# A two-layer graph network on one Trainium2 core: the second half of the first edge pass gathers float32 rows

## The chip, the core and the metric

The kernel runs on one core of one Trainium2 chip. A core has five engines that run side by side, each through its own instructions in order: PE (TensorE, matrix products), DVE (VectorE), ACT (ScalarE), POOL (GpSimd, which here issues the gathers) and SP (SyncE, which here issues the other DMAs). They wait for each other by semaphores. The metric is the device time of one execution in microseconds (us); lower is better.

## The reference: what is computed

The graph has 6250 nodes of 256 float32 features and 100,000 edges, sorted by destination. The edges crowd at low destinations, since `dst` is the square of a uniform number. Cut to what matters:

```python
def layer0(x, src, dst, weight, bias):                       # mean over the neighbours, then a linear layer
    agg = segment_sum(x[src], dst, n) / maximum(deg, 1)
    out = concatenate([x, agg], -1) @ weight
    return out / norm(out) + bias

x = layernorm(x + layer0(x, src, dst, ...))
x = layernorm(x + layer1(x, src, dst, ...))                  # the same edge sums again, then a mixture of 64 experts
```

The change touches only `segment_sum(x[src], dst)` of the first layer, the *first edge pass*.

## The kernel before, in words

**Two ways to sum edges.** The edges are cut into 782 chunks of 128. The first 288 chunks (dense destinations) become a matrix of edge counts, `adj_a` and `adj_b`, which later is multiplied by the node rows (`dense_product`, L420 to L444, product at L432). The other 494 chunks are *gathered*: an indirect DMA on POOL (`gather_rows`, L394 to L396) fetches the 128 source rows of a chunk, and PE multiplies them by a one-hot matrix that says which destination of a window each edge has. A group of 4 to 16 chunks shares one window and one accumulator `po`.

**Rows in three parts.** PE multiplies bfloat16 in one pass and float32 in several. So `three` splits every node row into three bfloat16 parts that add up to the float32 value, and writes them to `x3_rows` (1536 bytes a row instead of 1024). The first 64 steps (up to `xch`) can't wait for that table: they gather float32 rows from `x` with a float32 one-hot (`edge_rows`, L600 to L608) and one product (L667). From then on a chunk is gathered from `x3_rows` and takes three bfloat16 products with one bfloat16 one-hot (L685). Those one-hots are made four at a time by one DVE instruction (`near4`, L414 to L418). In both forms they are made `ahead = 4` steps early. There are eight row buffers, so POOL can be eight chunks ahead of PE.

**The order of the work.** The pass is one loop over the 494 steps (one gathered chunk each) inside a region in which the order of PE, DVE, ACT and SP is what the program wrote; POOL has little but gathers there. Side work is put between the steps by hand: `Track` spreads a list of work over a range of steps, `Steps` runs things some steps later. The side work by step, in `work`:

- up to step 318: the counts of the dense part and the degrees;
- 240 to 374: the dense product over `adj_a`; 322 to 374 also `by_destination` (L819, 392 very small products);
- 377 to 470: the dense product over `adj_b`; its node tiles `x3d` (192 KB) are loaded on SP (L896) into three buffers;
- from 321 on: the first layer itself (`layer1`, L504 to L570), one tile of 128 nodes every 3.5 steps (`B_GAP`), as soon as its edge sums are complete. It loads `xw` and `xb`, multiplies (L521), normalizes (ACT L535, L536, L546, L551; DVE L527 to L549), stores `x1_rows` (L552), splits the result in three parts (ACT L557, L564; DVE L561, L566) and stores them to `h3_rows` (L569; two buffers, so L557 of one tile waits for the store of the tile two before). ACT also clears the finished sums (L868).

At the end of a group, `group_end` copies `po` (ACT, `sums`, L632), PE transposes it three steps later (L402), DVE adds it to `acc` (L409). The last 8 groups (from group 46, step 457 on) do this with no lag. The second edge pass gathers `h3_rows`, so it begins when the last tile of the first layer has been stored.

Per step PE is given, in this order: the products of the step's chunk, then what `work` adds. ACT and DVE get the one-hot of the chunk four steps ahead first, then the rest.

Of the kernel before, what the change touches and what calls it, by code (L numbers as in the profile page):

```python
# [9 lines left out]
F32 = mybir.dt.float32  # L10
F16 = mybir.dt.float16
BF16 = mybir.dt.bfloat16
I32 = mybir.dt.int32
AF = mybir.ActivationFunctionType
OP = mybir.AluOpType
# [4 lines left out]
P = 128  # L20
N = 6250
D = 256
# [11 lines left out]
ACH, DCH = 216, 288  # L34
# [12 lines left out]
OHB = 4  # L47
# [13 lines left out]
def edge_groups(c0, c1, width, most):  # L61


    groups = []
    while c0 < c1:
        g = 1
        while g < min(most, c1 - c0):
            e0, e1 = c0 * P, (c0 + g + 1) * P
            per = E * E / (2.0 * N * e1)
            if N * (e1 / E) ** 2 - N * (e0 / E) ** 2 + 1 + 5 * (e1 - e0) ** 0.5 / per > width:  # L70
                break
            g += 1
        groups.append((c0, g))
        c0 += g
    return groups
# [4 lines left out]

FINE = 24
GGRP = edge_groups(DCH, NCH - FINE, P, 16) + edge_groups(NCH - FINE, NCH, P, 4)

AT_ONCE = max(i for i, (_, g) in enumerate(GGRP) if g >= 7)

# [60 lines left out]
def gnn_moe_kernel(  # L146
# [22 lines left out]
    nc = tc.nc  # L169
# [38 lines left out]
    ones = const.tile([P, P], F32, name="ones")  # L208
# [16 lines left out]
    with ExitStack() as gctx:  # L225
# [168 lines left out]
        def gather_rows(r, table, index):  # L394
            nc.gpsimd.indirect_dma_start(out=r, out_offset=None, in_=table,  # L395
                                         in_offset=bass.IndirectOffsetOnAxis(ap=index, axis=0))  # L396
# [186 lines left out]
        with ExitStack() as c:  # L583
# [4 lines left out]
            while GGRP[xgrp][0] - DCH < FIRST:  # L588
                xgrp += 1
            xch = GGRP[xgrp][0]  # L590
            assert xch <= DCH + FIRST + 16
            bufs = []
            rsq_out = wk.tile([P, NT], F32, name="rsq_out", bufs=1)
# [2 lines left out]
            steps = Steps()  # L596
            complete = [-1]
            free = dict(LAYER)

            def edge_rows(pool, ch, dt):  # L600
                oh = pool.tile([P, P], dt, name="oh")
# [35 lines left out]
            def gathered():  # L637
                ahead = 4
                ready = []

                def more_rows(ch):
                    if ch >= NCH:
                        return
                    i = ch - DCH
                    if ch < xch:
                        ready.append(edge_rows(ohf, ch, F32))
                    else:
                        if i % OHB == 0 or near_now[0] is None:
                            near_now[0] = near4(ohp, i - i % OHB)
                        ready.append(near_now[0][:, :, i % OHB])  # L650

                near_now = [None]
                with tc.tile_pool(name="stf", bufs=1, side="right") as stf, \
                        tc.tile_pool(name="ohf", bufs=6, side="right") as ohf:
                    bufs_f = [stf.tile([P, D + 1], F32, name=f"rows{i}") for i in range(7)]
                    for b in bufs_f:
                        nc.vector.memset(b[:, D:], 1.0)
                    for i in range(ahead):
                        more_rows(DCH + i)
                    for g_, (c0, g) in enumerate(GGRP[:xgrp]):  # L660
                        po = ps2.tile([P, D + 1], F32, name="po")
                        for ch in range(c0, c0 + g):
                            r = bufs_f[ch % 7]
                            gather_rows(r[:, :D], x, src_i[:, ch : ch + 1])
                            if ch + ahead < xch:
                                more_rows(ch + ahead)
                            nc.tensor.matmul(po, ready.pop(0), r, start=(ch == c0), stop=(ch == c0 + g - 1))  # L667
                            if ch == c0 + g - 1:
                                group_end(g_, po)
                            yield ch - DCH  # L670
                for i in range(ahead):
                    more_rows(xch + i)
                for g_, (c0, g) in enumerate(GGRP):
                    if g_ < xgrp:
                        continue
                    po = ps2.tile([P, D + 1], F32, name="po")
                    for ch in range(c0, c0 + g):
                        r = bufs[ch % nbuf]
                        gather_rows(r[:, : 3 * D], x3v, src_i[:, ch : ch + 1])
                        more_rows(ch + ahead)  # L680
                        oh = ready.pop(0)

                        for s in (2, 0, 1) if ch == c0 else (0, 1, 2):
                            w = D + (s == 2)
                            nc.tensor.matmul(po[:, :w], oh, r[:, s * D : s * D + w], start=(ch == c0 and s == 2),  # L685
                                             stop=(ch == c0 + g - 1 and s == 2))
                        if ch == c0 + g - 1:
                            group_end(g_, po)
                        yield ch - DCH
# [187 lines left out]
            with tc.manual_schedule(engines=ordered), ExitStack() as c1:  # L877
# [24 lines left out]
                def work(i):  # L902
                    nonlocal due, wl, psl, ohp, dense_done
                    if i == X_END + 9:
                        cx.close()
                        st = c1.enter_context(tc.tile_pool(name="st", bufs=1))
                        for k in range(nbuf):
                            bufs.append(st.tile([P, 3 * D + 1], BF16, name=f"rows3{k}"))
                            nc.vector.memset(bufs[k][:, 3 * D :], 1.0)
                        ohp = c1.enter_context(tc.tile_pool(name="ohp", bufs=3))  # L910
                        psh = hold.enter_context(tc.tile_pool(name="psh", bufs=1, space=PSUM))
                        ph[0] = psh.tile([P, NT], F32, name="ph")
                        ohc = hold.enter_context(tc.tile_pool(name="ohc", bufs=3))
                        psx = ca.enter_context(tc.tile_pool(name="psx1", bufs=1, space=PSUM))
                        psa[0] = ca.enter_context(tc.tile_pool(name="psa", bufs=3, space=PSUM))
                        wx = ca.enter_context(tc.tile_pool(name="wx", bufs=2))
                        every = counts(ohc, psa)
                        tracks.append(Track(every[:ACH], i, A_END - 4))
                        tracks.append(Track(every[ACH:], A_END + 1, END - 4))
                        tracks.append(Track([lambda t=t: staged(steps, own(wx, psx, t)) for t in range(NT)],  # L920
                                            i + 4, A_END - 12))
                        tracks.append(Track(sources(ohc), i + 8, END - 4))
                    if i == A_END:
                        ca.close()
                        psa[0] = cb.enter_context(tc.tile_pool(name="psb", bufs=2, space=PSUM))
                        tracks.append(dense(DA_END, adj_a, DENSE, 0))
                    if i == END:
                        cb.close()
                        with tc.tile_pool(name="psf", bufs=1, space=PSUM) as psf:
                            out_degrees(ph[0], psf)  # L930
                        hold.close()
                        wl = c1.enter_context(tc.tile_pool(name="wl", bufs=2))
                        psl = c1.enter_context(tc.tile_pool(name="psl", bufs=1, space=PSUM))
                        psg = cg.enter_context(tc.tile_pool(name="psg", bufs=1, space=PSUM))
                        tracks.append(Track(by_destination(psg), END + 4, DA_END))
                    for v in tracks:
                        v.at(i)
                    if i == DA_END + 3:
                        dense_done = EDGE // P
                        cd.close()  # L940
                        cg.close()
                        tracks.append(dense(DB_END, adj_b, MORE, EDGE))
                    if i == DB_END + 3:
                        dense_done = ND
                        cd.close()
                    if i > END + 2 and i >= due:
                        for t in todo:
                            if TLAST[t] <= complete[0] + 1 and (t >= ND or t < dense_done):
                                first_layer(t, wl, psl)
                                todo.remove(t)  # L950
                                due = max(due, i - 2) + (B_GAP if i < NG - 8 else 1)
                                break
                    steps.advance()
# [774 lines left out]
```

## Time and profile before

| What | Value |
|---|---|
| median of 4 runs | 2203.29 us (2199.85 to 2208.48) |
| the profiled execution | 2196.67 us |
| its span, first to last instruction | 2194.9 us |
| mean granted TensorE clock | 0.904 of full speed |
| PE busy | 1709.4 us (78%) |
| DVE / ACT / POOL busy | 1076.3 (49%) / 607.9 (28%) / 1208.1 us (55%) |
| first gather of the first edge pass | at 7.7 us |
| gather of step 332 / of the last step, 493 | at 520.42 / at 780.14 us |
| last store to `h3_rows` | at 817.3 us |

How to read it: busy times are sums over the whole span, and say little of a stage. The views used below are cut by time instead: busy time and clock of each engine in a stretch, who waited for whom in it (total us, times, longest), the DMA queues in it, and the instructions in order of time. An engine's "idle before" is put down to what ended it, its *releaser*.

### The profile page before, as it was taken

The page shows a single profiled execution, that of the slowest core. Times are in us where ns is not written, and L with a number is a line of the kernel's source. Part 1 is how long each engine was busy: PE and PEld are TensorE (multiplying, and loading weights), DVE is VectorE, ACT ScalarE, POOL GpSimd, SP SyncE. Part 2 cuts the span into 40 slices and gives each one's busy share as a digit, 9 for nine tenths or more (in the row PEclk, how much of TensorE's full clock was granted, in tenths as well). Part 3 has the DMA queues.
Part 4 walks back from the last instruction along what each step waited for, and adds up shares of the span by engine and source line. Part 5 has one row for each costly group of instructions (what it writes and reads, how often), then busy time and mean ns, then how long its engine had stood idle before and what let it go on. Part 6 is the DMA issues. An engine that isn't in the chain of part 4 may idle for free. (4 is left out here: it accounts for less than half of the span.)

```text
span 2194.9 us, 33723 instructions
## 1 busy us (share of the span) xinstructions
PE 1709.4 (78%) x9269; PEld 1207.1 (55%) x9341; DVE 1076.3 (49%) x4063; ACT 607.9 (28%) x1617; POOL 1208.1 (55%) x1391
## 2 busy tenths in 40 slices
PE   4688877788888738788667767766669998999797
PEld 2366555556655425454445444444347876787573
DVE  7666677675677661000245554535532233222398
ACT  8511235333444340000022222212212221222125
POOL 7766666666566516566666666666235554554100
PEclk8598899999999969999888899988869999999899
DMA  6766665567899836666666655555268887877353
GB/s 219 269 173 180 176 176 173 168 174 217 261 289 304 255 124 211 197 190 187 192 194 190 191 159 164 162 153 151 84 208 303 300 302 262 269 247 251 109 162 118
DMA packets 242215, 445.32 MB, mean 203 GB/s; under 512 B 35695, under 2 KB 165480, under 8 KB 242015
## 3 DMA queue, kind: packets, MB, share of 16 engines
q0 software_dynamic: 71808, 211.15, 32.9%
q1 hardware_dynamic: 167886, 230.37, 31.9%
q10 hardware_dynamic: 2320, 1.51, 0.2%
q8 instruction: 79, 1.29, 0.2%
q14 instruction: 122, 0.99, 0.2%
HBM read 377.20 MB, written 70.89 MB: 204 GB/s over the span
## 5 line engine op out<-in xcount | busy, mean ns | idle before, releaser
L395 POOL DMA_INDIRECT rows<-h_rows,src_i x494 | 477.7, 967 | 264.4 <-issue 101.3
L395 POOL DMA_INDIRECT rows<-x_rows,src_i x430 | 429.4, 999 | 246.0 <-issue 85.1
L1220 PE MATMUL both_po<-rows,oh 128*128 128x256 bf16 x1482 | 233.2, 290 | 124.8 <-ACT sums L1225 55.7
L1220 PEld LDWEIGHTS <-oh 128*128 128x128 bf16 x1482 | 166.3, 117 | 180.3 <-issue 143.4
L417 DVE TENSOR_TENSOR oh<-iota_lo,near 128x512 bf16<-128x512 bf16 x232 | 99.3, 430 | 306.7 <-PE both_po L1220 167.6
L685 PE MATMUL po<-rows,oh 128*128 128x256 bf16 (+1 forms) x1290 | 224.5, 287 | 3.5 <-issue 2.5
L1491 POOL DMA_INDIRECT core<-ob,ix x100 | 101.5, 1015 | 200.7 <-DVE ob L1490 184.9
L1489 PE MATMUL po<-w2t,h 128*128 128x256 f32 x800 | 190.7, 388 | 1.0 <-ACT h L1482 0.5
L1482 ACT ACTIVATE h<-ph,b1c 128x128 f32<-128x128 f32 (+1 forms) x288 | 94.4, 410 | 335.8 <-PE ph L1480 160.5
L779 PE MATMUL pa<-oha,ohl 128*128 128x490 bf16 x288 | 111.7, 394 | 77.8 <-issue 28.6
L1489 PEld LDWEIGHTS po<-w2t,h 128*128 128x128 f32 x800 | 150.3, 192 | 38.9 <-ACT h L1482 16.2
L685 PEld LDWEIGHTS <-oh 128*128 128x128 bf16 x1290 | 138.2, 119 | 49.1 <-issue 10.5
L1490 DVE TENSOR_TENSOR ob<-po,b2b 128x256 f32<-128x256 f32 x100 | 42.4, 424 | 227.2 <-PE po L1489 208.8
L758 DVE TENSOR_SCALAR oha<-iota_h,rel 128x490 bf16<-128x490 f16 x288 | 103.1, 366 | 96.7 <-PE po L685 38.1
L409 DVE TENSOR_TENSOR acc<-acc,pt 128x256 f32 x108 | 45.3, 420 | 151.2 <-PE both_po L1220 35.7
L1468 PE MATMUL ph<-xt,w1t 128*128 128x256 f32 x448 | 118.8, 406 | 0.0
L1225 ACT COPY sums<-both_po 128x256 f32<-128x256 f32 x54 | 20.1, 371 | 355.4 <-remote 209.1
L1468 PEld LDWEIGHTS ph<-xt,w1t 128*128 128x128 f32 x448 | 110.6, 326 | 5.6 <-issue 2.6
L1448 POOL DMA_INDIRECT xb<-xx_tok,ix x100 | 98.9, 989 | 25.0 <-issue 23.3
L432 PE MATMUL pd<-adj_b,x 128*128 128x448 bf16 x294 | 109.3, 372 | 1.7 <-issue 0.8
L432 PE MATMUL pd<-adj_a,x 128*128 128x512 bf16 x274 | 109.9, 401 | 0.7 <-issue 0.7
L1473 PE MATMUL ph<-w1t,xt 128*128 128x512 f32 x176 | 88.6, 604 | 0.5 <-DVE xt L1461 0.5
(343 smaller groups left out, 3363.4 us busy)
## 6 DMA issues: line engine op xcount, KB each, us to landing
w1t<-in_L_gnn_w_dram SPq DMA_DIRECT2D x72, 512.0 KB
w2t<-in_L_gnn_w_dram SPq DMA_DIRECT2D x72, 512.0 KB
x3d<-x_rows SPq DMA_DIRECT2D x98, 192.0 KB
core<-zero SPq DMA_DIRECT2D x7, 1792.0 KB
ys<-core SPq DMA_DIRECT2D x48, 256.0 KB
h_rows<-h SPq DMA_DIRECT2D x49, 192.0 KB
x<-h_rows SPq DMA_DIRECT2D x49, 192.0 KB
x_rows<-x SPq DMA_DIRECT2D x24, 384.0 KB
```

What stands on the lines that cost most here:

```text
L395: nc.gpsimd.indirect_dma_start(out=r, out_offset=None, in_=table, in_offset=bass.IndirectOffsetOnAxis(ap=index, axis=0))
L417: nc.vector.tensor_tensor(oh, iota_lo, near[:, None, c0 : c0 + OHB].to_broadcast([P, P, OHB]), op=OP.is_equal)
L432: nc.tensor.matmul(pd[h, w], side(x3, s, h), adj[:, t, a:b], start=(t == 0 and s == 0), stop=(t == NT - 1 and s == 2))
L685: nc.tensor.matmul(po[:, :w], oh, r[:, s * D : s * D + w], start=(ch == c0 and s == 2), stop=(ch == c0 + g - 1 and s == 2))
L758: nc.vector.tensor_scalar(oha, iota_h, rel[:, ch : ch + 1], None, op0=OP.is_equal)
L779: nc.tensor.matmul(pa[0].rearrange("p t w -> p (t w)"), low, places.pop(ch), start=first, stop=last)
L1220: nc.tensor.matmul(po, oh, r[:, :, s, :], start=(ch == c0 and s == 0), stop=(ch == c0 + g - 1 and s == 2))
L1448: nc.gpsimd.indirect_dma_start(out=xb[:, h, :], out_offset=None, in_=xx_tok, in_offset=bass.IndirectOffsetOnAxis(ap=ix[:, 0, h : h + 1], a ...
L1468: nc.tensor.matmul(ph[:, hc], w1m[:, c, hc, :], xt[:, c], start=(c == 0), stop=(c == 1))
L1482: nc.scalar.activation(h1[:, hc].rearrange("p h m -> p (h m)"), pre[hc].rearrange("p h m -> p (h m)") if k == 0 else pre[hc], AF.Gelu, bia ...
L1489: nc.tensor.matmul(po, h1[:, hc, h, :], w2t[:, hc * D : (hc + 1) * D], start=(hc == 0), stop=(hc == 3))
L1491: i = nc.gpsimd.indirect_dma_start(out=core, out_offset=bass.IndirectOffsetOnAxis(ap=ix[:, 1, h : h + 1], axis=0), in_=ob[:, h, :], in_off ...
```

## The change

From the first group that begins at step 326 or later, which is step 332 (`tgrp`, `tch`), to the end of the pass at step 493, a chunk is gathered as the 128 float32 rows of `x` (1024 bytes each) and takes one float32 product 257 columns wide, whose last column, set to one, counts the edges. That is 162 chunks. Their one-hots are float32 too, so a buffer that held four bfloat16 one-hots now holds two: `plain_rows` makes two at a time, the first on ACT by two activations (Abs, Relu), the second on DVE by one comparison, after a DVE copy of the two columns of places. The row buffers are seen as float32; their column of ones is set by DVE at each buffer's first use (8 times). The dense products and the second edge pass still use the three-part tables.

```diff
+PLAIN = 326
...
+            tgrp = next(g_ for g_, (c0, _) in enumerate(GGRP) if c0 - DCH >= PLAIN)
+            tch = GGRP[tgrp][0]
...
+            def plain_rows(c0):
+                v = ohp.tile([P, P, OHB], BF16, name="oh4").rearrange("p a b -> p (a b)").bitcast(F32)
+                place = ohp.tile([P, 2], F32, name="place2")
+                i = c0 - DCH
+                nc.vector.tensor_copy(place, near[:, i : i + 2])
+                two = [v[:, k * P : (k + 1) * P] for k in range(2)]
+                nc.scalar.activation(two[0], iota_row, AF.Abs, bias=place[:, 0:1], scale=-1.0)
+                nc.scalar.activation(two[0], two[0], AF.Relu, bias=ones[:, 0:1], scale=-1.0)
+                nc.vector.tensor_scalar(two[1], iota_row, place[:, 1:2], None, op0=OP.is_equal)
+                return two
...
-                    if ch < xch:
+                    if ch >= tch:
+                        if (ch - tch) % 2 == 0:
+                            ready.extend(plain_rows(ch))
+                    elif ch < xch:
...
+                        if g_ >= tgrp:
+                            r = r[:, : 2 * (D + 1)].bitcast(F32)
+                            if ch < tch + nbuf:
+                                nc.vector.memset(r[:, D:], 1.0)
+                            gather_rows(r[:, :D], x, src_i[:, ch : ch + 1])
+                            more_rows(ch + ahead)
+                            nc.tensor.matmul(po, ready.pop(0), r, start=(ch == c0), stop=(ch == c0 + g - 1))
+                            if ch == c0 + g - 1:
+                                group_end(g_, po)
+                            yield ch - DCH
+                            continue
...
-                            bufs.append(st.tile([P, 3 * D + 1], BF16, name=f"rows3{k}"))
+                            bufs.append(st.tile([P, 3 * D + 2], BF16, name=f"rows3{k}"))
```

## The prediction

> **What bounds the kernel now.** I read the times by stage first, since the page's shares are means over the whole span. Columns: stretch, length, then busy time of PE, PEld, DVE, ACT and POOL, the granted clock, the DMA engines' share, GB/s.
>
> ```profile
> 520.00:590.00 70.00, 63.41 (x613) 46.19 (x625) 44.71 (x169) 30.73 (x96) 42.19 (x44) 0.93 0.84 253
> 590.00:745.00 155.00, 128.09 (x793) 88.67 (x793) 110.49 (x418) 72.74 (x232) 96.37 (x99) 0.98 0.91 291
> 745.00:800.00 55.00, 32.15 (x151) 21.82 (x149) 36.71 (x138) 25.09 (x79) 20.04 (x21) 0.81 0.55 170
> ```
>
> The changed steps lie here. Step 332 is gathered at 520.4 us, and the three stretches are stage A (dense product over `adj_a`, 42 changed steps), B (over `adj_b`, 99 gathers in it) and C (no dense product, the remaining 21). In A, PE is busy 63.4 of 70 us at a clock of 0.93: PE is the bound. In B nothing is full: PE is idle 27 us of 155, the DMA engines are at 0.91. In C every engine is half idle, so a chain of waits sets the time. The second pass starts after the last store to `h_rows` at 817 us, so what these stages lose or gain is passed on whole.
>
> Next, who waits in B: PE's waits, then those of ACT, then of POOL.
>
> ```profile
> PE pd L432 <- DMA x3d<-x_rows: 13.9, 14, 2.1
> PE pg L830 <- DVE mv L544: 4.2, 1, 4.2
> PE pt L402 <- issue: 3.5, 4, 1.1
> PE pd L432 <- issue: 3.4, 6, 1.0
> ```
>
> ```profile
> ACT h L557 <- DMA h_rows<-h: 21.1, 10, 4.7
> ACT h L557 <- issue: 20.7, 13, 3.7
> ```
>
> ```profile
> POOL rows L395 <- PE po L685: 26.2, 25, 3.0
> ```
>
> PE waits 17.3 us in front of L432, nearly all for node tiles of the dense product, and never for gathered rows: POOL is the one that waits for PE to free a row buffer. ACT stands 42 us in front of L557, until an old store of `h` has landed. So traffic costs something in B, but not through the gathers' own arrival.
>
> **The change, part by part.**
>
> *Products.* The trace has both kinds, in the same stretch (start, length, engine, line):
>
> ```profile
> 661.47 0.73 PE L432 MATMUL pd<-adj_b,x3d 128*128 128x448 bf16 x3
> 662.04 1.03 PE L521 MATMUL po<-w,acc 128*128 128x256 f32 x4
> 662.90 0.49 PE L685 MATMUL po<-rows,oh 128*128 128x256 bf16 x3
> 663.23 0.73 PE L432 MATMUL pd<-adj_b,x3d 128*128 128x448 bf16 x3
> ```
>
> From start to start, three bfloat16 products of 256 columns take 663.23 - 662.90 = 0.33 us. Two float32 products of 256 columns (four records) take 662.90 - 662.04 = 0.86, so one takes 0.43. "One in place of three" is therefore 0.10 us longer, not shorter. Divided by the clock: A 42 x 0.10/0.93 = 4.5 us, B 99 x 0.10/0.98 = 10.1, C 21 x 0.10/0.81 = 2.6, together **+17 us** of PE. All of it is on the path in A. In B it can be paid for by PE's idle time only if the waits that make that idle time get shorter.
>
> A float32 weight load is longer too (row L521, mean 205 ns, against 118 ns in row L685), but L521's 0.86 us already holds its loads, so they are hidden behind products. The Trainium skill, page "TensorE: Matmul & The Clock Gate", section "Weight-path perf modes", says that the fast weight load is off for FP32 inputs. That speaks against the change; if nothing hid the loads, two of 0.2 us a chunk would add 65 us to the sum. The pair of L521 shows that they are hidden.
>
> *Traffic.* The queue of the gathers, in B and in the opening stretch from 45 to 97 us, where rows are float32:
>
> ```profile
> q0 software_dynamic: 6311, 19.38, 40.7%
> ```
>
> ```profile
> q0 software_dynamic: 1734, 4.75, 28.7%
> ```
>
> A three-part gather costs 0.407 x 16 x 155 / 99 = 10.2 engine-us, a float32 one 0.287 x 16 x 52 / 37 = 6.5. B saves 99 x 3.7/16 = 23 us of DMA time, and its share falls from 0.91 to (141 - 23)/155 = 0.76. What that buys is the 17.3 us at L432, between 0 (if SP, where each `x3d` load stands behind stores that wait for ACT, is what makes them late) and 17.3. The nearest row is stage A: at a share of 0.84 PE waits 0.2 us there for the same loads, though it uses them a third more slowly. I take **-12 us**. POOL's cost per gather stays, 0.95 us and 0.3 between two; that floor of 1.25 a step lies under today's 155/99 = 1.57.
>
> *One-hots.* Before, DVE makes four in 0.42 us (L417) with room for twelve. Now each pair takes two ACT instructions, one DVE copy and one DVE comparison, with room for six. The opening stage shows the prices:
>
> ```profile
> L607 ACT ACTIVATE oh<-oh,ones 128x128 f32<-128x128 f32 x36 | 14.5, 402 | 2.5 <-ACT oh L606 1.4
> L606 ACT ACTIVATE oh<-iota_row,rel 128x128 f32<-128x128 f32 x36 | 14.3, 396 | 5.5 <-PE po L667 3.9 <-issue 1.7
> L604 DVE TENSOR_SCALAR oh<-iota_row,rel 128x128 f32<-128x128 f32 x24 | 6.5, 270 | 2.6 <-PE po L667 2.2 <-issue 0.4
> ```
>
> Two activations take 0.73 us from one pair's start to the next one's (19.03 to 19.76 us). So ACT gets 81 x 0.73 = 59 us of work, 36 of it in B: from 72.7 to 109 of 155 (0.70). DVE loses 25 x 0.42 = 10 us in B and gets 50 x (0.27 + 0.15 for the copy, as in rows of that size) = 21: from 110 to 121 (0.78). Both have the time on average. But these engines go through their lists in order, and the one-hots now stand behind L557's waits for a store of up to 4.7 us, while PE is only four steps (some 6 us) away. What is late then is the product itself and, behind it on PE, the dense products. The nearest row is the opening stage (8 to 98 us), where the same one-hots are made with ACT 64.3/90 = 0.71 and DVE 70.2/90 = 0.78 busy, just the shares worked out above. There PE waited 5.6 us for `oh` and 5.7 for another ACT result in front of the product, 11.3 us in 61 chunks. All of that on 162 chunks is 30 us; the lower end is 0, since ACT's 42 us at L557 can take in the 36. The longest of those waits fell in the first loads, so I take less than half: **+12 us**.
>
> The skill has a rule against this, page "ScalarE: Activation LUTs", section "Rules for kernel authors": take VectorE, not ScalarE, for relu and its like. The rows agree in direction (0.73 us against 0.27). By that rule the pair would cost DVE 22 us more and ACT nothing; the sum here goes by what was written.
>
> *The rest.* Eight settings of the column of ones stand on DVE in the step that uses them, not four ahead; DVE is idle 25 of 70 us in A, so 0 to 3 us. In C, `sums` (L632) stands behind a pair of activations at the end of 6 groups, and PE waits for `sums` there already; but ACT makes the pair while PE does the group's last product, so 0 to 6 x 0.73 = 4 us. I take **+1** for both together. ACT's function tables don't change: the built order of the changed kernel has five table loads, as before has. SP's and POOL's orders are the same.
>
> *Sum:* 17 - 12 + 12 + 1 = **+18 us**. The profiled execution took 2196.67 us (span 2194.9), so it would be 2214.7. It lies 6.6 us under the median of the runs, 2203.29; added to that, the forecast is **2221 us**.
>
> **The rivals.**
>
> *Faster: traffic is the real bound of B.* The waits at L557 and L432 are both waits for transfers and hold up ACT, SP and PE alike. If they go, and the one-hots fit into the freed time of ACT, all 27 us of PE's idle time in B can go: -27 + 17 = -10 us, with a few us more if the modelled ends of the products hide idle time, 2190 us. For it: 0.91 in B. Against it: in A, PE pays with nothing to gain, and each x3d load also waits on SP. It decides if PE's wait at L432 disappears and none for `oh` takes its place.
>
> *No change.* The price of the products (17) is just met by the wait at L432 (17.3), and ACT's idle time takes in the one-hots: 2203.
>
> *Slower by far: ACT becomes the bound.* If the wait at L557 doesn't shrink by what ACT now does in between, ACT adds its work to the path: 36 us in B and up to 15 in A and 8 in C, 59 in all; with the 17 of the products partly beside it, some 45 us, 2248. It decides from the point at which ACT's new 0.37 us a step no longer fits into its idle time, 82 of 155 us in B, of which 42 are at L557.
>
> *That it doesn't do what it says* is ruled out: the built order has 162 float32 products and 162 gathers from `x` in place of 486 and 162.
>
> **How the numbers follow.** Forecast (+8 to +35) 0.48, faster 0.20, no change 0.20, ACT-bound 0.12. About 0.3% (6.6 us) is what a measurement of this kernel can tell from no change. So faster 0.20, same 0.20, slower 0.60. The range goes from inside the faster case, 2192, to the ACT-bound price, 2248, and leaves out about half of each of these two.
>
> **What would show it.** In the profile after: a product of `oh4` 0.43 us from start to start, not 0.33; gathers of 6.5 engine-us; a DMA share near 0.76 in the stage of `adj_b`; PE's wait for `x3d` down to about 5 us; a new wait of PE for `oh` on ACT or DVE of 10 to 15 us; ACT at 0.7. The forecast is wrong if PE doesn't wait for one-hots (then it is the no-change case, or faster), or if ACT hardly has idle time left (then the slow one).

## The result, and the profile after

The changed kernel takes 2213.92 us (median of 40 runs, 2201.56 to 2224.34), the kernel before 2206.26 us beside it (66 runs). The ratio is 1.0035 [1.0024, 1.0045]: slower by 7.7 us, where +18 was forecast. The profiled execution took 2213.0 us (span 2211.3, clock 0.907).

Lines have moved: in the changed kernel the dense product is L434, the plain product L704, the copy of places L609, Abs and Relu L611 and L612, the comparison L613, the `h` activations of the first layer L559 and L566, `sums` L648, the transpose L404. Step 332 is gathered at 525.6 us, so the stages lie at 525 to 597 (A), 597 to 755 (B) and 755 to 812 (C). Busy times by stage (stretch, length, PE, PEld, DVE, ACT, POOL, clock, DMA share, GB/s):

```profile
525.00:597.00 72.00, 65.15 (x571) 45.68 (x582) 48.63 (x207) 44.69 (x136) 41.27 (x43) 0.98 0.69 206
597.00:755.00 158.00, 137.46 (x691) 92.91 (x693) 121.20 (x492) 105.35 (x329) 94.55 (x99) 0.97 0.81 246
755.00:812.00 57.00, 36.38 (x135) 25.45 (x132) 40.48 (x158) 33.78 (x105) 20.05 (x21) 0.83 0.45 138
```

PE has 9 us more work in B, ACT 33 more, DVE 11 more, and the DMA engines 0.10 less: all of it near what was worked out (ACT 105.35/158 = 0.67, DVE 0.77). Yet every stretch is longer by only 2 or 3 us, 7 in all. PE's waits in B:

```profile
PE pg L860 <- DVE col L859: 4.4, 1, 4.4
PE pd L434 <- DMA x3d<-x_rows: 3.8, 5, 1.8
PE pt L404 <- ACT sm L548: 3.1, 2, 1.9
PE pt L404 <- issue: 2.3, 2, 1.5
PE pd L434 <- issue: 2.0, 2, 1.6
```

The wait for node tiles fell from 17.3 to 5.8 us, as forecast. A wait of the product L704 for a one-hot, which was forecast with 10 to 15 us, isn't there in B. In A there is one, of 1.7 us, and one for which the profile shows no releaser (the same view for 525 to 597 us):

```profile
PE po L704 <- issue: 2.7, 1, 2.7
PE po L704 <- DVE place L609: 1.7, 1, 1.7
```

ACT's waits in B, and then from C to the start of the second pass:

```profile
ACT h L559 <- DMA h_rows<-h: 13.6, 8, 3.8
ACT h L559 <- issue: 5.9, 7, 3.2
ACT oh L611 <- issue: 5.8, 5, 2.0
ACT oh L611 <- PE pd L434: 4.3, 2, 2.2
ACT oh L611 <- DVE place L609: 4.0, 3, 2.4
ACT oh L611 <- DVE sm L550: 3.6, 3, 2.0
```

```profile
ACT h L559 <- DMA h_rows<-h: 9.8, 5, 2.6
ACT oh L611 <- DVE place L609: 7.7, 4, 3.0
```

Here is the new thing. ACT's 42 us in front of the first `h` activation shrank to 19.5, and in part of their place ACT stands in front of its own Abs, 17.7 us in the four rows above. Of these, 7.6 are put to DVE (the copy of the places, or what DVE does ahead of it), 4.3 to PE, and 5.8 to nothing that the profile shows. The prices of the parts, from the order of PE's instructions in B and from the gathers' queue in the same stretch:

```profile
641.37 0.73 PE L434 MATMUL pd<-adj_b,x3d 128*128 128x448 bf16 x3
641.93 0.60 PE L704 MATMUL po<-rows,oh 128*128 128x257 f32 x2
642.37 0.73 PE L434 MATMUL pd<-adj_b,x3d 128*128 128x448 bf16 x3
```

```profile
q0 software_dynamic: 4743, 12.97, 30.3%
```

A float32 product takes 642.37 - 641.93 = 0.44 us from start to start (forecast 0.43). A gather takes 0.303 x 16 x 158/99 = 7.7 engine-us (forecast 6.5, before 10.2).

### The profile page after: what moved, and what is told of

Its sections match the earlier page's. It is cut to its first block, busy times and chain, and to the rows that moved or that the text cites. A ratio compares the mean times of both kernels' runs of the same rounds, so it can differ in the third digit from the quotient of the medians.

```text
span 2211.3 us, 33835 instructions
## 1 busy us (share of the span) xinstructions
PE 1723.0 (78%) x9108; PEld 1212.0 (55%) x9179; DVE 1094.4 (49%) x4192; ACT 663.2 (30%) x1779; POOL 1198.8 (54%) x1391
## 5 line engine op out<-in xcount | busy, mean ns | idle before, releaser
L397 POOL DMA_INDIRECT rows<-x_rows,src_i x268 | 267.6, 998 | 152.1 <-issue 51.1
L397 POOL DMA_INDIRECT rows<-in_x_dram,src_i x226 | 226.6, 1003 | 136.6 <-PE po L704 53.7
L1250 PEld LDWEIGHTS <-oh 128*128 128x128 bf16 x1482 | 167.4, 118 | 190.0 <-issue 154.0
L419 DVE TENSOR_TENSOR oh<-iota_lo,near 128x512 bf16<-128x512 bf16 x191 | 82.5, 434 | 307.4 <-PE both_po L1250 166.9
L809 PE MATMUL pa<-oha,ohl 128*128 128x490 bf16 x288 | 110.5, 388 | 86.6 <-issue 40.3
L715 PE MATMUL po<-rows,oh 128*128 128x256 bf16 (+1 forms) x804 | 140.0, 285 | 2.3 <-issue 1.9
L411 DVE TENSOR_TENSOR acc<-acc,pt 128x256 f32 x108 | 45.2, 419 | 136.1 <-PE both_po L1250 32.3
L434 PE MATMUL pd<-adj_b,x 128*128 128x448 bf16 x294 | 109.6, 373 | 2.7 <-issue 1.8
L434 PE MATMUL pd<-adj_a,x 128*128 128x512 bf16 x274 | 109.8, 401 | 0.2 <-issue 0.2
L704 PE MATMUL po<-rows,oh 128*128 128x257 f32 x324 | 102.7, 409 | 4.7 <-issue 2.7
```

The costliest lines, as they stand in the source:

```text
L434: nc.tensor.matmul(pd[h, w], side(x3, s, h), adj[:, t, a:b], start=(t == 0 and s == 0), stop=(t == NT - 1 and s == 2))
L809: nc.tensor.matmul(pa[0].rearrange("p t w -> p (t w)"), low, places.pop(ch), start=first, stop=last)
L1250: nc.tensor.matmul(po, oh, r[:, :, s, :], start=(ch == c0 and s == 0), stop=(ch == c0 + g - 1 and s == 2))
```

## The experiments

The theory at first was the prediction's own sum, with the one-hots as its weak term; its rivals were that products, traffic or ACT's added work alone decide. The second theory, which came up after the first four runs and is tested by itself in the last group, is that **neither products nor traffic count, and the loss is ACT's Abs waiting, in ACT's fixed order, for DVE's copy of the places**. The runs came in three groups, each beside runs of before on the same chip, whose medians were 2209.30, 2187.14 and 2190.04 us; all ratios are to those (12 runs, 11 for `e4_onehots_only`, against 35).

### Traffic alone, and traffic undone

`e1_traffic_only` is before with only two of the three parts gathered (1024 bytes) from step 332 on; the third part is whatever the buffer held. Its table of shorter rows is made by 7 copies at steps 100 to 160.

```diff
+                        if ch - DCH >= 332:
+                            gather_rows(r[:, : 2 * D], x2_rows, src_i[:, ch : ch + 1])
```

> The kernel before, but from step 332 on a gather fetches only the first two of the three parts (1024 bytes a row, from a table that is copied from the three-part table at steps 100 to 160); the third part of a chunk is left as an older chunk had it. One-hots and three bfloat16 products as before. Theory 1 (traffic is worth 12 to 17 us in the stage of adj_b, through the loads of x3d and the stores of h): from the gather of step 332 to the first gather of the second pass 283 to 289 us where before shows 300.1, PE's wait for x3d under 6 us, total 10 to 17 us under before apart from what the copies cost early (0 to 5 us). Theory 2 (the wait for x3d got short after the change only because PE itself came later): 297 to 301 us, total no better than before.

Measured: 0.9985 [0.9962, 1.0008], that is -3.3 us with 0 inside. PE's waits in B (596 to 747 us):

```profile
PE pd L433 <- issue: 5.8, 7, 1.8
PE pd L433 <- DMA x3d<-x_rows: 5.4, 6, 1.7
```

The wait for node tiles fell from 17.3 to 11.2 us and the DMA share from 0.91 to 0.83, and B stayed at 150.7 us from the gather of step 374 to that of 470 (before: 150.6). From the gather of step 332 to the second pass it took 296.9 us, where before took 300.1: the forecast of "traffic without effect" (297 to 301), not the other (283 to 289). The copies lie ahead of that stretch, but inside the ratio.

`e2_padded` is the change with rows padded to 1536 bytes, so that its traffic is that of before; the padded table is made by 14 copies much earlier. `e3_copy_only` is the change with these copies and nothing else.

```diff
-                            gather_rows(r[:, :D], x, src_i[:, ch : ch + 1])
+                            gather_rows(r[:, : 3 * P], pad_rows, src_i[:, ch : ch + 1])
```

> The changed kernel, but its float32 rows are gathered from a table of rows padded to 1536 bytes, so traffic is that of before, and products and one-hots are those of the change. Theory 1: the gain of 12 is given back, steps 332 to the second pass take 315 to 323 us (after: 306.4), PE waits 12 us or more for x3d, total 9 to 16 us over the control with the copies alone. Theory 2 (traffic without effect): same as the control within 3 us.

> The changed kernel with the copies that fill the padded table (9.6 MB at steps 100 to 160), which nothing reads: the control of the padded one. All theories: 0 to 5 us over the changed kernel, all of it before step 332, and 305 to 308 us from there to the second pass.

Measured: 1.0031 [1.0014, 1.0047] and 1.0033 [1.0016, 1.0051]. Against each other (medians of 12 runs each, resampled) the padded one takes 1.0002 [0.998, 1.002] of its control: with or without the saved bytes, the changed kernel takes the same time within some 5 us, where 9 to 16 were forecast if traffic counted. The wait for node tiles did come back, 9.2 us in B against 3.0. The padded kernel's profile is 316.6 us from step 332 to the second pass, in the range of the theory that traffic counts, but that execution lay 15 us above the median of its runs. The saving of traffic is worth nothing that these runs can tell.

### The one-hots alone

`e4_onehots_only` is before, all its rows and products as they were, plus the change's copy, activations and comparison, into buffers of their own that nobody reads.

```diff
                         gather_rows(r[:, : 3 * D], x3v, src_i[:, ch : ch + 1])
+                        if ch - DCH >= 332 - ahead and ch % 2 == 0 and ch + ahead < NCH:
+                            plain_rows(ch + ahead)
```

> The kernel before, with the float32 one-hots made as in the change (two activations, a copy and a comparison a pair, from step 328 on) and not used: ACT's and DVE's added work alone, DVE's four-at-a-time one-hots still there. Theory 1 (the added work is mostly hidden, and comes out only as sums copied later, in front of PE's transposes): 302 to 307 us from step 332 to the second pass, total 2 to 6 us over before. Rival (the one-hots' work is the large cost, as the prediction had it): 310 us or more, total 10 to 15 over before.

Measured: 1.0035 [1.0013, 1.0056]: by itself it gives a slowdown as large as the change's, 7.7 us. That lies between the two forecasts (2 to 6, and 10 to 15). PE reads none of these one-hots, so it isn't a wait of PE for them. Nor is it mainly the recorded theory, sums copied later: PE's wait for `sums` from step 470 to the second pass is 14.9 us, against 13.5 before. The Abs in the changed steps (group line of ACT, 524 to 826 us: busy, mean ns | idle just before them, and what ended it):

```profile
L607 ACT ACTIVATE oh<-iota_row,place 128x128 f32<-128x128 f32 x81 | 32.0, 395 | 41.1 <-DVE place L605 24.0 <-issue 10.9 <-DVE xb L530 1.9
```

ACT idles 41 us in front of 32 us of work, most of it for the copy of two columns.

### The products alone, and ACT's work alone

`e5_extra_product` is before with a fourth bfloat16 product, by zeros, in every chunk from step 332 on.

```diff
+                        if ch - DCH >= 332:
+                            order = (2, 0, 1, 1) if ch == c0 else (0, 1, 1, 2)
...
+                                nc.tensor.matmul(po[:, :D], oh, nought, start=False, stop=False)
```

> The kernel before, with a fourth bfloat16 product of 256 columns (by zeros) in every chunk from step 332 on: 0.11 us more of PE a chunk, as the float32 product costs more than the three, with traffic and one-hots as before. If PE's time is the bound (the prediction's term of 17 us): A 72 to 73 us, B 158 to 161 us against 150.6, total 12 to 17 us over before. If PE's idle time in B takes it in, because something else sets the pace there: A up to 4 us longer, B within 3 us, total 0 to 5 us over before.

Measured: 1.0000 [0.9981, 1.0019]. Stage B of before and of this kernel, both cut from the gather of step 374 to that of 470:

```profile
589.00:739.00 150.00, 124.82 (x775) 86.56 (x774) 107.75 (x407) 69.88 (x223) 93.46 (x96) 0.98 0.91 293
```

```profile
583.00:732.00 149.00, 134.53 (x874) 97.82 (x872) 108.07 (x407) 69.83 (x224) 93.57 (x96) 0.98 0.93 295
```

PE has 9.7 us more to do and the stage isn't longer. Even A, where PE is busy for nine tenths, took 69.2 us and not 68.2, where 42 x 0.11/0.93 = 5 more would be added by price (a third of the 0.33 us that three products take). A is the weaker case, though: PE's busy time rose there by 2.6 us alone (61.9 to 64.5), and the clock granted in this profile's A was 0.95 and not 0.93.

`e6_act_only` is before with the two activations for each pair of chunks, their places read from columns of a float32 table that was ready long before; no DVE instruction is added.

```diff
+                v = ohp2.tile([P, P], F32, name="oh8")
+                r = rel[:, c0 % 200 : c0 % 200 + 1]
+                nc.scalar.activation(v, iota_row, AF.Abs, bias=r, scale=-1.0)
+                nc.scalar.activation(v, v, AF.Relu, bias=ones[:, 0:1], scale=-1.0)
```

> The kernel before, with two unused activations a pair of chunks from step 328 on (ACT's share of the change's one-hots, with places that are ready long before), nothing added on DVE. If ACT's added 0.73 us a pair is what costs: total 5 to 9 us over before, like the one-hots alone (7.7). If it is DVE's copy and comparison, or ACT's wait for DVE's copy: 0 to 3 us.

Measured: 1.0006 [0.9989, 1.0023]. The same 162 activations as in `e4_onehots_only`, and hardly a cost. Their group line (516 to 815 us):

```profile
L603 ACT ACTIVATE oh<-iota_row,rel 128x128 f32<-128x128 f32 x81 | 31.8, 393 | 0.0
```

No idle time in front of them: with nothing to wait for, they fill ACT's free time.

### The change with another one-hot, and a fourth buffer for node tiles

`e7_pair` is the change with both one-hots of a pair made by one DVE comparison, straight from the bfloat16 places: no copy, no activation.

```diff
-                nc.vector.tensor_copy(place, near[:, i : i + 2])
-                nc.scalar.activation(two[0], iota_row, AF.Abs, bias=place[:, 0:1], scale=-1.0)
-                nc.scalar.activation(two[0], two[0], AF.Relu, bias=ones[:, 0:1], scale=-1.0)
-                nc.vector.tensor_scalar(two[1], iota_row, place[:, 1:2], None, op0=OP.is_equal)
+                nc.vector.tensor_tensor(oh, iota_lo[:, :, :2], near[:, None, i : i + 2].to_broadcast([P, P, 2]),
+                                        op=OP.is_equal)
```

> The changed kernel with both one-hots of a pair made by one DVE comparison of 256 columns straight from the table of places: no activation, no copy of the places. If the one-hots' work is what the change costs: within 3 us of before, so 5 to 9 under the changed kernel, and a little under before if traffic is worth anything. If the products and the traffic decide: as the changed kernel, 6 to 10 us over before.

Measured: 1.0006 [0.9988, 1.0024]. All 162 float32 products and gathers are in it, so products and traffic together cost nothing that can be told from 0. One such comparison of 256 columns takes 0.421 us; the change's DVE part is a copy of 0.186 and a comparison of 0.304 us (means in `e9_change_again`).

`e8_x3d4` is before with four buffers for `x3d` in place of three.

> The kernel before with four buffers for the node tiles x3d in place of three, so that their loads can be issued two steps earlier. If PE's wait for x3d (17.3 us in the stage of adj_b) is what holds that stage: B 136 to 142 us, total 8 to 14 us under before. If that wait only fills a time that ACT's and SP's chain of the first layer sets: the wait goes and another one comes, B within 3 us, total within 3 us of before.

Measured: 1.0007 [0.9992, 1.0022]. PE's waits in B (581 to 732 us):

```profile
PE pt L402 <- ACT sums L632: 8.1, 3, 4.8
PE pg L830 <- DVE col L829: 3.9, 1, 3.9
PE po L521 <- issue: 3.8, 3, 2.7
PE pt L402 <- ACT sm L536: 3.1, 3, 1.3
PE pt L402 <- issue: 2.0, 3, 0.9
PE pd L432 <- DMA x3d<-x_rows: 1.4, 1, 1.4
```

The wait at L432, which the forecast counted as up to 17 us to be won, and took as 12, is nearly gone, and the idle time stands in front of other lines instead. B took 151.1 us.

### The wait itself

The last group takes the wait away in two ways, and its neighbour, the wait for a free buffer, in a third. All stand beside the change itself on their chip.

`e9_change_again` is the change, unaltered.

> The change itself once more, so that its ratio is had on the same chip and beside the same runs of before as the next three (its ratio over all its runs was 1.0035, and the two experiments that cost nothing ran on another chip). Both theories: 1.002 to 1.005. If it is 1.001 or less, the slowdown is not the same on every chip, and the one-comparison version's 1.0006 proves nothing.

Measured: 1.0045 [1.0024, 1.0067]. A ratio given here isn't simply the quotient of two medians: that would be 1.0036 for this run and 1.0003, 1.0002 and 1.0017 for the next three, lower by 0.0009 to 0.0016. The comparisons with the change itself don't depend on before.

`e10_early_places` is the change with one copy of all places, ahead of the changed steps, into columns of `rel` that are free by then.

```diff
-                nc.vector.tensor_copy(place, near[:, i : i + 2])
+                place = rel[:, c0 - tch : c0 - tch + 2]
...
                     if i == END:
+                        nc.vector.tensor_copy(rel[:, : NCH - tch], near[:, tch - DCH : NCH - DCH])
```

> The change, but all places are turned to float32 by one VectorE copy ahead of the first changed chunk, into columns of rel that are free by then: the Abs has no copy of its own pair to wait for, and VectorE issues 81 copies fewer. Theory 'ScalarE's Abs waits in its queue for VectorE's copy': 0.999 to 1.001, the waits of the Abs for the copy gone. Rival 'the Abs waits for the buffer, that is for TensorE's product of six chunks before' or 'the instructions themselves on two engines': 1.002 to 1.005 as the change, and the same waits of the Abs under another releaser.

Measured: 1.0012 [0.9989, 1.0034], with the point just above the 0.999 to 1.001 that the theory forecast. Against `e9_change_again` on the same chip (medians of 12 runs each, resampled) the change is slower by 1.0033 [1.0017, 1.0056], some 7 us, about all that it had lost. The Abs of the two kernels, first the change (517 to 826 us), then this one (516 to 821):

```profile
L611 ACT ACTIVATE oh<-iota_row,place 128x128 f32<-128x128 f32 x81 | 32.1, 397 | 46.3 <-DVE place L609 28.2 <-PE po L704 5.1 <-PE po L523 3.0
```

```profile
L609 ACT ACTIVATE oh<-iota_row,rel 128x128 f32<-128x128 f32 x81 | 32.0, 395 | 13.9 <-PE po L702 9.5 <-PE pg L847 2.7 <-PE pd L434 1.6
```

The wait for the copy is gone and the wait for a buffer, 9.5 us, has stayed without doing much harm.

`e11_all_vector` is the change with both one-hots by DVE comparisons with a column of places; the copy stays, no activation is issued.

```diff
-                nc.scalar.activation(two[0], iota_row, AF.Abs, bias=place[:, 0:1], scale=-1.0)
-                nc.scalar.activation(two[0], two[0], AF.Relu, bias=ones[:, 0:1], scale=-1.0)
-                nc.vector.tensor_scalar(two[1], iota_row, place[:, 1:2], None, op0=OP.is_equal)
+                for k in range(2):
+                    nc.vector.tensor_scalar(two[k], iota_row, place[:, k : k + 1], None, op0=OP.is_equal)
```

> The change, but both one-hots of a pair by VectorE's comparison with a column of places (the copy stays, no activation is issued for one-hots): ScalarE has no part in it. VectorE does 0.16 + 2 x 0.29 us a pair, 0.29 more than in the change. Theory 'the wait between ScalarE and VectorE': 0.999 to 1.001, VectorE's own order does the rest. Rival 'VectorE's added instructions hold the first layer': 1.004 to 1.008, more than the change.

Measured: 1.0018 [0.9997, 1.0040]. DVE has the most work of all versions (127.59 us in B against 116.68 in `e9_change_again`), and it is faster than the change, not slower: the change against it is 1.0034 [1.0008, 1.0050]. So the copy and DVE's load aren't the bulk of the cost. An effect of half the size isn't excluded: 1.0018 lies above the 0.999 to 1.001 that the theory forecast.

`e12_five_buffers` is the change with five one-hot buffers in place of three.

```diff
+                pool = (ohp, ohp2)[(c0 - tch) // 2 % 5 % 2]
+                v = pool.tile([P, P, OHB], BF16, name="oh4").rearrange("p a b -> p (a b)").bitcast(F32)
+                place = pool.tile([P, 2], F32, name="place2")
```

> The change with five one-hot buffers in place of three: an Abs or a copy waits for no product of TensorE's until ten chunks back. Theory 'the Abs waits for VectorE's copy': as the change, 1.002 to 1.005. Rival 'the wait for the buffer': 0.999 to 1.001, and the Abs's wait for pd and po gone.

Measured: 1.0033 [1.0010, 1.0056]; the change against it is 1.0019 [1.0006, 1.0032], so a part may lie in the buffers, but not all of it. Its Abs still idle (514 to 818 us):

```profile
L612 ACT ACTIVATE oh<-iota_row,place 128x128 f32<-128x128 f32 x81 | 32.0, 395 | 42.2 <-DVE place L610 22.0 <-issue 11.4 <-DVE sm L550 6.2
```

### One such wait, and where the time goes

The timeline of ACT and DVE in stage C of `e9_change_again` (start, length, engine, line, what; in brackets the idle time before and what ended it):

```profile
752.62 0.29 ACT L548 ACTIVATE sm<-mv,eps_col 128x1 f32<-128x1 f32 x1
...
753.82 0.42 DVE L411 TENSOR_TENSOR acc<-acc,pt 128x256 f32 x1 [0.75 <-PE pt L641]
754.16 0.20 DVE L650 TENSOR_TENSOR deg<-deg,pt 128x49 f32<-128x49 f32 x1
754.27 0.48 DVE L563 SCALAR_TENSOR_TENSOR rv<-o,rsq_out,h 128x256 f32<-128x256 f32 x1
...
754.93 1.13 DVE L443 TENSOR_TENSOR acc<-acc,pd 128x448 f32<-128x448 f32 x2
...
755.98 0.16 DVE L609 CAST place<-near 128x2 f32<-128x2 bf16 x1
...
756.18 0.40 ACT L611 ACTIVATE oh<-iota_row,place 128x128 f32<-128x128 f32 x1 [3.26 <-DVE place L609]
...
756.61 0.40 ACT L612 ACTIVATE oh<-oh,ones 128x128 f32<-128x128 f32 x1
...
756.92 0.39 ACT L566 CAST h<-rv 128x256 bf16<-128x256 f32 x1
```

ACT is done with L548 at 752.91. Next in its order is an Abs, whose places DVE copies only at 755.98, behind an addition that waits for PE (L411), the `rv` of the first layer (L563) and two additions of the dense product (L443). What stands behind the Abs on ACT, the second part of `h` (L566), has had its `rv` since 754.75 and runs at 756.92, 2.2 us late. A one-hot that is wanted four steps on holds up a result that is wanted at once; its copy is a small thing, but it joins ACT's queue to the end of DVE's.

In B such a delay may be made up (not shown). At the end of the pass POOL waits for the last `h` to be stored before the second pass begins. POOL's wait there, in the change (`e9_change_again`) and with early places:

```profile
POOL iota_b L1095 <- DMA h_rows<-h: 42.9, 1, 42.9
```

```profile
POOL iota_b L1094 <- DMA h_rows<-h: 38.2, 1, 38.2
```

Cutting every profile at the gathers of steps 332 and 470 and at the first gather of the second pass gives this table (us; one profile each, and that of `e2_padded` was the slowest of its runs):

| Kernel | ratio | A and B | C to the second pass |
|---|---|---|---|
| before | 1 | 218.8 | 81.4 |
| e1 traffic alone | 0.9985 | 217.4 | 79.6 |
| e5 products alone | 1.0000 | 218.9 | 81.0 |
| e6 activations alone | 1.0006 | 219.3 | 79.7 |
| e7 change, one comparison | 1.0006 | 217.7 | 78.3 |
| e8 four `x3d` | 1.0007 | 218.8 | 80.4 |
| e10 change, early places | 1.0012 | 224.2 | 80.0 |
| e11 change, all on DVE | 1.0018 | 221.4 | 81.2 |
| e3 change and copies | 1.0033 | 222.3 | 85.1 |
| e12 change, five buffers | 1.0033 | 218.9 | 85.3 |
| e2 change, padded | 1.0031 | 229.0 | 87.5 |
| e4 one-hots alone | 1.0035 | 226.5 | 86.6 |
| change | 1.0035 | 223.3 | 83.0 |
| e9 change again | 1.0045 | 221.7 | 87.8 |

The last column parts the two kinds without an overlap: 78.3 to 81.4 us (mean 80.2) where no Abs waits for a copy, 83.0 to 87.8 (mean 85.9) where one does. That is 5.7 of the 7.7 us. In A and B the means are 219.6 and 223.6, but the kinds overlap (217.4 to 224.2 against 218.9 to 229.0), so how much of the loss lies there stays unsettled. The profiles of before and of the change alone would say otherwise: there 4.6 us more lie in A and B, and 1.7 in the last column. One profile of each kernel can't place the loss; only the means over the two kinds speak for the end of the pass.

## Why the prediction was right, and where its sum was off

The direction and the likeliest case (slower, through ACT and DVE going through their lists in order) were right; the size, +18 against +7.7, was not, and two of the three large terms come out as nothing that these runs can tell from 0. That these two nearly cancelled, and so left the forecast near the measured time, was luck; the one-hots' own +12 lies nearer to the 7.7 than the whole sum does.

**What bounds the kernel.** "In A, PE 63.4 of 70 us busy: PE is the bound" isn't borne out: in `e5_extra_product` A took 1 us more for products priced at 5 us. With the clock of that profile at 0.95 it isn't refuted either. "In C a chain of waits sets the time" and "what these stages lose is passed on whole" fit the table above, whose last column holds 5.7 us of the loss in the means.

**Products, +17.** The price was right (0.44 us measured), the place was wrong: B had the room, and in the total no loss shows. `e5_extra_product` and `e7_pair` give 0; the upper ends of their intervals allow 0.19% and 0.24%, 4 to 5 us.

**Traffic, -12.** The wait fell as forecast (L432's 17.3 to 5.8, forecast about 5; DMA share 0.81, forecast 0.76), but traffic is only part of why. With the saved traffic alone (`e1_traffic_only`) it is 11.2 us; with the added products alone and not a byte saved (`e5_extra_product`) it is 9.3 us in B; in the change without the saving (`e2_padded`) 10.9. A likely reason, not tested, is that a PE with more to do comes later to the same loads. And the wait was not on the path that sets the end: `e1_traffic_only` -3.3 [-8.4, +1.8] us, padded rows no change, and `e8_x3d4` removes the wait and gains nothing. The sum took a wait of PE for a gain of the kernel.

**One-hots, +12.** The right term, and all that can be shown of the loss, but by another way. It was priced as PE waiting for one-hots, after the opening stage, where PE's order has little else; here PE's waits in front of the plain product are 4.6 us in all, in A alone, and only 1.7 of them are put to the making of a one-hot. The late thing is ACT's next work behind the Abs. The text had seen the head of it, "these engines go through their lists in order, and the one-hots now stand behind L557's waits", but asked only who waits for the one-hot, and not what waits behind it. That 42 us at L557 could take in ACT's work fits `e6_act_only` (1.0006); but that ACT stood there for an old store of `h` is shown for 21.1 of them alone, the other 20.7 having no releaser in the profile.

**The rest, +1.** It wasn't measured alone. PE's wait for `sums` in C didn't grow: 13.5 us before, 8.6 after. For a column of ones PE waits once, 1.2 us in `e9_change_again`, and not at all in the first profile of the change.

**The rivals.** Traffic as the real bound of B: no, by `e1_traffic_only` and `e8_x3d4`. ACT as the bound: no, by `e6_act_only`. "No change" is what the products and the traffic give together, and what the change gives once the copy is out of the way (`e7_pair`, `e10_early_places`), though not because 17 and 17 cancel. The condition set for a wrong forecast, "if PE doesn't wait for one-hots, then it is the no-change case", was too narrow: PE hardly waited, and the time rose.

In the prediction the rule of the Trainium skill, page "ScalarE: Activation LUTs", section "Rules for kernel authors", to take VectorE for relu, was set against the rows. `e11_all_vector` agrees with it in direction (1.0018 against 1.0045), but not for the reason that the page gives, speed per element: ACT's activations cost nothing that can be told from 0 while they wait for nothing (`e6_act_only`).

**What stays open.** What sets the pace of B, 1.57 us a step. More PE work, less traffic, another `x3d` buffer, 31 us more of ACT and 20 more of DVE each left it between 149.7 and 152.5 us; where an Abs waits for a copy, B took 149.4 to 157.7. No single engine's load sets it, then; a chain through several of them, or the hand-written order, is only argued. No version tried is faster than before beyond its interval.

## What to carry to other kernels

A new instruction can cost twice: its time, and what stands behind it in its engine's order while it waits. Before putting a small producer on one engine and its consumer on another, look at what the producer is queued behind and what is queued behind the consumer; if the input can be made long before, or both sit on one engine, that wait can go, as it did in `e10_early_places`, `e11_all_vector` and `e7_pair`. A wait of the busiest engine is worth what the path to the end gives for it, which a run with that wait removed, or with that engine's work raised, tells and the busy share doesn't.

## What was not expected of the hardware

- A stage with PE busy for 124.8 of 150 us took 9.7 us more of PE's busy time into none (149.0). One with 61.9 of 68.2 took 2.6 more into 1.0 us, at a granted clock of 0.95 in place of 0.93.
- DVE's comparison of 128 columns takes 0.304 us, one of 256 columns 0.421, the copy of 2 columns 0.186: two columns cost nearly half of 256. The Trainium skill, page "VectorE: DVE Perf Modes", section "The TRN2 errata — SBUF-src ops pay a fixed extra latency per instruction", says that each instruction pays a fixed share and that many small ones pay it each; the rows agree in kind.
- A gather of 1024-byte rows took 7.7 engine-us in B and 6.5 in the opening stretch, though the DMA engines were busier in the opening (0.95 from 45 to 97 us, against 0.81). Why is not shown.
- The medians of the same kernel (before) on three chips were 2187 to 2209 us, 1% apart and three times the effect studied here. Only ratios to runs on the same chip could show it.
